# Two graph-attention layers on one core: attention scores computed key-major, denominators by a matmul with ones

## The chip, the cores and the metric

The kernel runs on one core of a Trainium2 chip. A core has a matrix engine (TensorE, "PE" in the profile, with its weight loads listed as "PEld"), a vector engine (VectorE, "DVE"), an activation engine (ScalarE, "ACT"), a general engine (GpSimd, "POOL") and a queue for transfers (SyncE, "SP"). Each engine works through its own instructions in order, and they wait for each other by semaphores. The metric is the device time of one execution in microseconds. Three runs of the kernel before took 3482.77, 3483.33 and 3484.8 us; the median is 3483.33.

## The reference

The input is 64 batches of 256 tokens with 512 features, all in 32-bit floats, and one 256 x 256 adjacency matrix. Layer 0 normalises, takes the positive part, multiplies by the adjacency and by a weight. Layer 1 is attention with 8 heads of 64 features; the mask added to the scores comes from the same adjacency.

```python
def _L0_gnn_ref(x, adj, weight, bias):
    y = jnp.einsum('nm,bmd->bnd', adj, x)
    return jnp.einsum('bnd,do->bno', y, weight) + bias

def _L1_gnn_ref(x, adj, Wq, bq, Wk, bk, Wv, bv, Wo, bo):
    q = (x @ Wq + bq).reshape(b, n, H, HD)
    ...
    scores = jnp.einsum('bqhd,bkhd->bhqk', q, k) / jnp.sqrt(jnp.float32(HD))
    scores = scores + (1.0 - adj)[None, None, :, :] * -1000000000.0
    attn = jax.nn.softmax(scores, axis=-1)
    out = jnp.einsum('bhqk,bkhd->bqhd', attn, v).reshape(b, n, d)
    return out @ Wo + bo

h = jnp.maximum(_layernorm(x, axis=-1), 0.0)
x = x + _L0_gnn_ref(h, adj, L0_gnn_weight, L0_gnn_bias)
h = jnp.maximum(_layernorm(x, axis=-1), 0.0)
x = x + _L1_gnn_ref(h, adj, L1_gnn_Wq, ...)
```

The adjacency is between 0 and 1, not symmetric in its values, and no row is all zero (its diagonal is at least 0.05).

## The kernel before

The 64 batches are taken in 32 groups of two. One group has 512 tokens: four tiles of 128 tokens by 512 features. All weights stay in SBUF.

`pre(g)` is layer 0 and the q, k and v of layer 1 of one group. It loads nothing itself; it takes the group's x tile, computes mean and variance on DVE (`moments`, L120 to L123), the two scales (`norm_scales`, L111 to L118: a tensor-scalar on DVE, a power on POOL, a product on DVE), the normalised positive part `h` on ACT (L134), and adds the bias on POOL (L135). Then come steps that each fill one PSUM bank of 512 columns and are evacuated by ACT or DVE: four `py` (adjacency times h, copied to `yT` by ACT), four `pw` (times the layer-0 weight, added to x by DVE, with the second layer's moments), four `h1` on ACT with four transposes `ph` each and a DVE copy to `h1T`, four `pq`, four `pk` (evacuated by ACT with the bias), and four `pv` (evacuated by DVE). `post(g)` is the output projection: four `po`, each added to `x1` by DVE, and a store for each batch.

Attention works in units: one pair of heads of one batch, eight units in a group. `softmax` (L207 to L229) makes query-major scores `sc`: queries on the partitions, keys along the row, two heads and two query tiles, so 1024 columns in two PSUM banks. The two heads lie on the two 64-partition halves of q and k, so their matmuls use the two row halves of the array. DVE scales and adds the mask (L218), then takes each row's maximum (L221). ACT takes the exponential with that maximum as bias, four instructions of 256 columns, which also give the row sums (L224). DVE takes the reciprocals of the four sums (L227), and POOL multiplies the four blocks by them (L229). `transpose` (L231 to L243) turns the eight 128 x 128 blocks on TensorE, because the product with v needs the keys on the partitions, and copies them from PSUM to `aT`, one head on ACT and one on DVE. `attend` (L245 to L259) multiplies with v; the two heads write the two 64-partition halves of a PSUM bank `pav` (tag `po`), using the two column halves of the array. When both batches of a head pair are in it, DVE copies it to `oT`.

The order is written out in the loop at the end, and a scheduler then places the instructions on each engine, so that neighbouring pieces can interleave. In a group's loop, `softmax` runs two units ahead of `transpose` and `attend`, and between them the generator `fill` is advanced: it holds the steps of `post(g - 1)` followed by those of `pre(g + 1)`. What is left of `fill` runs at the group's end.

PSUM has eight banks: three for the steps (tag `mm`), two for one unit's scores (`sc`), two for the transposes (`tr`), one for `pav` (`po`).

Of the kernel before, what the change touches and what calls it, by code (L numbers as in the profile page):

```python
# [8 lines left out]
F32 = mybir.dt.float32  # L9
AF = mybir.ActivationFunctionType  # L10
ALU = mybir.AluOpType
AX = mybir.AxisListType


@with_exitstack
def kernel(
# [17 lines left out]
    P = 128  # L34
    B, N, D = x.shape
    H, HD = 8, D // 8
    DC = D // P            # chunks of the feature dimension
    NT = N // P            # token tiles of one batch
    GB = 2                 # batches of one group
    T = GB * NT            # token tiles of one group  # L40
    GN = GB * N            # tokens of one group
    NG = B // GB
    HP = H // 2            # head pairs: two heads fill one 128-feature chunk
    EPS = 1e-5
    SCALE = 1.0 / 8.0
    assert (N, D, HD, GN) == (256, 512, 64, 512)

    const = ctx.enter_context(tc.tile_pool(name="const", bufs=1))
    xpool = ctx.enter_context(tc.tile_pool(name="x", bufs=2))
    act = ctx.enter_context(tc.tile_pool(name="act", bufs=1))  # L50
    qkv = ctx.enter_context(tc.tile_pool(name="qkv", bufs=2))
    att = ctx.enter_context(tc.tile_pool(name="att", bufs=2))
    small = ctx.enter_context(tc.tile_pool(name="small", bufs=4))
    psum = ctx.enter_context(tc.tile_pool(name="psum", bufs=1, space=bass.MemoryType.PSUM))
# [11 lines left out]

    def load_weight(w, name):
        t = const.tile([P, DC, D], F32, name=name)
        nc.scalar.dma_start(t, w.rearrange("(c p) o -> p c o", p=P))  # L69
        return t  # L70

    def load_row(b, name):
        t = const.tile([P, D], F32, name=name)
        nc.scalar.dma_start(t, bass.AP(tensor=b.tensor, offset=b.offset, ap=[[0, P], [1, D]]))  # L74
        return t

    def load_column(b, name):
        t = const.tile([P, DC], F32, name=name)
        nc.scalar.dma_start(t, b.rearrange("(c p) -> p c", p=P))  # L79
        return t  # L80

    w0_sb = load_weight(w0, "w0_sb")
    b0_r = load_row(b0, "b0_r")
    wq_sb = load_weight(wq, "wq_sb")
    bq_c = load_column(bq, "bq_c")
    wk_sb = load_weight(wk, "wk_sb")
    bk_c = load_column(bk, "bk_c")
    wv_sb = load_weight(wv, "wv_sb")
    bv_r = load_row(bv, "bv_r")
    wo_sb = load_weight(wo, "wo_sb")  # L90
    bo_r = load_row(bo, "bo_r")
# [5 lines left out]
    nc.vector.memset(mhalf, -0.5)  # L97

    # adjT[m, k, n] = adj[n, k * 128 + m]
    adjT = const.tile([P, NT, N], F32, name="adjT")  # L100
    pa = psum.tile([P, NT, N], F32, tag="mm", name="pa", bufs=3)
# [4 lines left out]
    mask = const.tile([P, NT, N], F32, name="mask")  # L106
    nc.vector.tensor_scalar(mask, adj_sb, -1.0, 1.0, op0=ALU.mult, op1=ALU.add)
    nc.vector.tensor_scalar(mask, mask, -1000000000.0, None, op0=ALU.mult)
    mask_b = mask.rearrange("p t m -> p (t m)")[:, None, :].to_broadcast([P, 2, NT * N])

    def norm_scales(mv, name):  # L111
        """From (mean, variance) of T token tiles: 1 / sqrt(variance + eps), and -mean times that."""
        rs = small.tile([P, T], F32, tag="rs", name=f"rs_{name}")
        nb = small.tile([P, T], F32, tag="nb", name=f"nb_{name}")
        nc.vector.tensor_scalar(rs, mv[:, :, 1], EPS, None, op0=ALU.add)
        nc.gpsimd.tensor_tensor(rs, rs, mhalf, op=ALU.pow)
        nc.vector.scalar_tensor_tensor(nb, mv[:, :, 0], -1.0, rs, op0=ALU.mult, op1=ALU.mult)
        return rs, nb  # L118

    def moments(mv, t, src, name):  # L120
        st = small.tile([P, nc.vector.BN_STATS_DIM], F32, tag="st", name=f"st_{name}_{t}")
        nc.vector.bn_stats(st, src)
        nc.vector.bn_aggr(mv[:, t, :], st)  # L123

    def pre(g):
        """Layer 0 and the q, k and v of layer 1, in steps of one PSUM bank each."""
        xt = XT.pop(g)
        mv = small.tile([P, T, 2], F32, tag="mv", name=f"mv0_{g}")
        for t in range(T):
            moments(mv, t, xt[:, t, :], f"0_{g}")  # L130
        rs, nb = norm_scales(mv, f"0_{g}")
# [3 lines left out]
        nc.gpsimd.tensor_tensor(xt, xt, b0_r[:, None, :].to_broadcast([P, T, D]), op=ALU.add)  # L135

        # yT = (adj @ h) transposed
        yT = act.tile([P, DC, GN], F32, tag="yT", name=f"yT_{g}")
        for d in range(DC):
            ps = psum.tile([P, GN], F32, tag="mm", name=f"py_{g}_{d}", bufs=3)  # L140
            for b in range(GB):
                for k in range(NT):
                    nc.tensor.matmul(ps[:, b * N:(b + 1) * N], h[:, b * NT + k, d * P:(d + 1) * P],  # L143
                                     adjT[:, k, :], start=(k == 0), stop=(k == NT - 1))
            nc.scalar.copy(yT[:, d, :], ps)
            yield
# [3 lines left out]
        for t in range(T):  # L150
            ps = psum.tile([P, D], F32, tag="mm", name=f"pw_{g}_{t}", bufs=3)
# [4 lines left out]
            moments(mv, t, x1[:, t, :], f"1_{g}")  # L156
            yield

        rs, nb = norm_scales(mv, f"1_{g}")
# [106 lines left out]
    for _ in pre(0):  # L266
        pass
# [56 lines left out]
```

## Time and profile before

| what | value |
|---|---|
| runs shown | 3482.77, 3483.33, 3484.8 us |
| profiled execution, span from first to last instruction | 3481.1 us |
| granted TensorE clock, mean | 0.999 |
| POOL, scaling by the reciprocals (L229), 1024 times | 928.2 us busy |
| ACT, exponentials (L224), 1024 times | 507.2 us busy |
| ACT, reading their sums, 1024 times | 191.3 us busy |
| DVE, scale and mask (L218), 256 times | 311.3 us busy |
| DVE, row maxima (L221), 256 times | 309.6 us busy |
| DVE and ACT, copies of the transposes (L243, L241), 256 each | 175.9 and 148.7 us busy |
| DVE, copy of pav to oT (L259), 128 times | 88.6 us busy |
| POOL, bias added to 128 x 2048 (L135, L170), 32 each | 144.7 and 144.6 us busy |
| HBM traffic | 21 GB/s over the span |

The page gives no separate total for the profiled execution; its span is 2.2 us under the median of the runs. Rows of the page name the line, engine, operation, the tiles written and read, shapes, count, then busy time in total, the mean of one in ns, and the idle time before such instructions with who ended it. Matmul records overlap each other, so their mean is longer than the slot that one takes; the spacing of blocks in the chain of waits is the better price. A matmul of 32-bit floats is two records.

### The profile page before, as it was taken

The page shows a single profiled execution, that of the slowest core. Times are in us where ns is not written, and L with a number is a line of the kernel's source. Part 1 is how long each engine was busy: PE and PEld are TensorE (multiplying, and loading weights), DVE is VectorE, ACT ScalarE, POOL GpSimd, SP SyncE. Part 2 cuts the span into 40 slices and gives each one's busy share as a digit, 9 for nine tenths or more (in the row PEclk, how much of TensorE's full clock was granted, in tenths as well). Part 3 has the DMA queues.
Part 4 walks back from the last instruction along what each step waited for, and adds up shares of the span by engine and source line. Part 5 has one row for each costly group of instructions (what it writes and reads, how often), then busy time and mean ns, then how long its engine had stood idle before and what let it go on. Part 6 is the DMA issues. An engine that isn't in the chain of part 4 may idle for free.

```text
span 3481.1 us, 33533 instructions
## 1 busy us (share of the span) xinstructions
PE 3434.9 (99%) x12804; PEld 1774.1 (51%) x12804; DVE 1537.4 (44%) x2308; ACT 1092.9 (31%) x2945; POOL 1281.7 (37%) x1158
## 2 busy tenths in 40 slices
PE   6999999999999999999999999999999999999999
PEld 3555545555455554555545555545555455554554
DVE  1453444444445434455344453444544445434444
ACT  2332323323333233332233322333323333223332
POOL 1443334324334234343333433334424334233333
PEclk9999999999999999999999999999999999999999
DMA  3000000000000000000000000000000000000000
GB/s 109 13 25 13 25 13 25 25 25 13 13 25 25 25 13 19 19 25 25 13 25 13 25 25 16 21 13 25 25 25 13 18 19 25 25 13 19 7 13 25
DMA packets 38863, 75.54 MB, mean 22 GB/s; under 512 B 2736, under 2 KB 2992, under 8 KB 38704
## 3 DMA queue, kind: packets, MB, share of 16 engines
q1 hardware_dynamic: 34304, 67.12, 5.5%
q10 hardware_dynamic: 4400, 6.30, 0.5%
q8 instruction: 101, 1.65, 0.2%
q14 instruction: 58, 0.48, 0.0%
HBM read 39.85 MB, written 33.55 MB: 21 GB/s over the span
## 4 chain that ended last, share of the span: by engine, by line
PE 97%; ACT 1%; POOL 1%; ACTq 1%; issue 0%; DVE 0%; POOLq 0%; DVEq 0%
PE po L196 13%; PE pq L177 13%; PE pv L185 13%; PE pk L177 13%; PE pw L153 13%; PE pav L253 9%; PE sc L213 9%; PE py L143 7%; PE tr L238 6%; PE ph L168 2%; POOL a L229 1%; ACT aT L241 1%; ACTq L69 0%; ACTq L74 0%; ACTq L79 0%
## 5 line engine op out<-in xcount | busy, mean ns | idle before, releaser
L229 POOL TENSOR_SCALAR a<-a,rden 128x256 f32<-128x256 f32 x1024 | 928.2, 926 | 1770.5 <-PE po L196 946.6
L224 ACT ACTIVATE a<-a,nmax 128x256 f32<-128x256 f32 x1024 | 507.2, 496 | 552.6 <-DVE nmax L221 545.4
L196 PE MATMUL po<-wo_sb,oT 128*128 128x512 f32 x1024 | 470.7, 602 | 0.0
L177 PE MATMUL pk<-h1T,wk_sb 128*128 128x512 f32 x1024 | 453.0, 595 | 0.0
L153 PE MATMUL pw<-w_sb,yT 128*128 128x512 f32 x1024 | 453.0, 595 | 0.0
L185 PE MATMUL pv<-wv_sb,h1T 128*128 128x512 f32 x1024 | 453.0, 595 | 0.0
L177 PE MATMUL pq<-h1T,wq_sb 128*128 128x512 f32 x1024 | 449.7, 597 | 0.8 <-DVE h1T L169 0.8
L241 ACT COPY aT<-tr 128x512 f32<-128x512 f32 x256 | 148.7, 581 | 893.5 <-PE tr L238 893.5
L218 DVE SCALAR_TENSOR_TENSOR a<-sc,mask 128x1024 f32<-128x1024 f32 x256 | 311.3, 1216 | 260.4 <-PE sc L213 259.2
L253 PE MATMUL pav<-aT,v 128*64 128x256 f32 x2048 | 355.0, 392 | 9.3 <-ACT aT L241 9.3
L213 PE MATMUL sc<-kT,qT 64*128 64x256 f32 x2048 | 343.2, 407 | 0.0
L177 PEld LDWEIGHTS pq<-h1T,wq_sb 128*128 128x128 f32 x1024 | 192.5, 191 | 243.7 <-issue 230.7
L221 DVE TENSOR_REDUCE nmax<-a 128x4 f32<-128x1024 f32 x256 | 309.6, 1209 | 4.3
L185 PEld LDWEIGHTS pv<-wv_sb,h1T 128*128 128x128 f32 x1024 | 189.6, 190 | 227.1 <-issue 227.1
L177 PEld LDWEIGHTS pk<-h1T,wk_sb 128*128 128x128 f32 x1024 | 189.6, 190 | 225.5 <-issue 215.6
L153 PEld LDWEIGHTS pw<-w_sb,yT 128*128 128x128 f32 x1024 | 189.6, 190 | 225.1 <-issue 217.4
L196 PEld LDWEIGHTS po<-wo_sb,oT 128*128 128x128 f32 x1024 | 183.8, 190 | 213.5 <-issue 213.0
L238 PEld LDWEIGHTS tr<-ident,a 128*128 128x128 f32 x2048 | 231.8, 141 | 109.2 <-issue 82.8
L238 PE MATMUL tr<-ident,a 128*128 128x128 f32 x2048 | 273.0, 276 | 3.7 <-POOL a L229 3.7
L253 PEld LDWEIGHTS pav<-aT,v 128*64 128x64 f32 x2048 | 163.5, 136 | 216.8 <-issue 136.2
L243 DVE COPY aT<-tr 128x512 f32<-128x512 f32 x256 | 175.9, 687 | 219.6 <-PE tr L238 219.6
L213 PEld LDWEIGHTS sc<-kT,qT 64*128 64x128 f32 x2048 | 191.6, 185 | 155.9 <-issue 85.3
(37 smaller groups left out, 2358.3 us busy)
## 6 DMA issues: line engine op xcount, KB each, us to landing
xt<-in_x_dram SPq DMA_DIRECT2D x32, 1024.0 KB, 5.2
out_dram<-x SPq DMA_DIRECT2D x64, 512.0 KB, 2.8
w_sb<-in_L_gnn_weight_dram ACTq DMA_DIRECT2D x1, 1024.0 KB, 11.6
wq_sb<-in_L_gnn_Wq_dram ACTq DMA_DIRECT2D x1, 1024.0 KB, 14.8
wk_sb<-in_L_gnn_Wk_dram ACTq DMA_DIRECT2D x1, 1024.0 KB, 15.5
wv_sb<-in_L_gnn_Wv_dram ACTq DMA_DIRECT2D x1, 1024.0 KB, 10.0
wo_sb<-in_L_gnn_Wo_dram ACTq DMA_DIRECT2D x1, 1024.0 KB, 9.6
adj_sb<-in_adj_dram ACTq DMA_DIRECT2D x1, 256.0 KB, 5.6
```

The source lines that it names most:

```text
L143: nc.tensor.matmul(ps[:, b * N:(b + 1) * N], h[:, b * NT + k, d * P:(d + 1) * P], adjT[:, k, :], start=(k == 0), stop=(k == NT - 1))
L153: nc.tensor.matmul(ps, yT[:, d, t * P:(t + 1) * P], w0_sb[:, d, :], start=(d == 0), stop=(d == DC - 1))
L177: nc.tensor.matmul(ps, w[:, d, m * P:(m + 1) * P], h1T[:, d, :], start=(d == 0), stop=(d == DC - 1))
L185: nc.tensor.matmul(ps, h1T[:, d, t * P:(t + 1) * P], wv_sb[:, d, :], start=(d == 0), stop=(d == DC - 1))
L196: nc.tensor.matmul(ps, oT[:, c, t * P:(t + 1) * P], wo_sb[:, c, :], start=(c == 0), stop=(c == HP - 1))
L213: nc.tensor.matmul(ps[:, j, t * N:(t + 1) * N], Q[g][j * HD:(j + 1) * HD, hp, b * N + t * P:b * N + (t + 1) * P], K[g][j * HD:(j + 1) * HD ...
L218: nc.vector.scalar_tensor_tensor(a.rearrange("p (j t) m -> p j (t m)", j=2), ps, SCALE, mask_b, op0=ALU.mult, op1=ALU.add)
L221: nc.vector.tensor_reduce(nmax, a, AX.X, ALU.max, negate=True)
L224: nc.scalar.activation(a[:, i, :], a[:, i, :], AF.Exp, bias=nmax[:, i:i + 1], accum_out=den[:, i:i + 1])
L229: nc.gpsimd.tensor_scalar(a[:, i, :], a[:, i, :], rden[:, i:i + 1], None, op0=ALU.mult)
L238: nc.tensor.transpose(ps[:, k, t * P:(t + 1) * P], a[:, j * NT + t, k * P:(k + 1) * P], ident)
L253: nc.tensor.matmul(PO[hp][j * HD:(j + 1) * HD, b * N:(b + 1) * N], V[g][:, b * NT + k, h * HD:(h + 1) * HD], aT[:, j, k, :], start=(k == 0 ...
```

## The change

Layer 0, the projections and the weights are computed as before. In the attention:

- `score` makes the scores key-major: keys on the partitions, queries along the row (k is the stationary side, q the moving one). The product with v can read the exponentials directly. `transpose`, its PSUM banks and its copies are gone.
- The row maximum is no longer of the scores. A constant `top`, made once, holds for each query the largest mask value of its row, spread over all partitions. `shift` is the DVE operation of before with the transposed mask, and then a subtraction of `top` on POOL (128 x 1024). `exponent` is one ACT instruction of 1024 columns without sums, and then a POOL addition of the two key tiles (128 x 512).
- `attend` handles both batches of a head pair: eight matmuls with v, over k first and the heads inside, and four matmuls of a 128 x 64 matrix of ones with the added exponentials, which give the denominators in a bank `pden` (tag `pd`), each on the 64 partitions that its head's output has. ACT copies them to SBUF and sums them along the row into `stats`; DVE takes the reciprocal of 128 x 512 values in four pieces; DVE multiplies `pav` by it into `oT`; ACT sums the reciprocals into `stats`.
- The loop goes over head pairs: `softmax` of the next pair, `attend` of this one and `fill` advance in turn, five times. The first pair's `softmax` of a group runs at the end of the group before. `pre` has one more step border.
- PSUM: two banks for the steps, four for scores (two buffers), one `po`, one `pd`. Buffers of `a`: four.
- At the end `stats` is compared with a bound of 1e22; one matmul counts the partitions over it, the count is read into a register, and if it is over zero, `general_path` computes everything again with the row maxima, in a loop over the batches with the instructions of the kernel before.

```diff
-    def softmax(g, u):
-        ...
-        nc.vector.tensor_reduce(nmax, a, AX.X, ALU.max, negate=True)
-        ...
-        for i in range(2 * NT):
-            nc.scalar.activation(a[:, i, :], a[:, i, :], AF.Exp, bias=nmax[:, i:i + 1],
-                                 accum_out=den[:, i:i + 1])
-        ...
-        for i in range(2 * NT):
-            nc.gpsimd.tensor_scalar(a[:, i, :], a[:, i, :], rden[:, i:i + 1], None, op0=ALU.mult)
-    def transpose(g, u):
-        ...
+    maskT = const.tile([P, NT, N], F32, name="maskT")
+    nc.vector.tensor_scalar(maskT, adjT, -1.0, 1.0, op0=ALU.mult, op1=ALU.add)
+    nc.vector.tensor_scalar(maskT, maskT, MASKED, None, op0=ALU.mult)
+    ...
+    top_b = top[:, None, :].to_broadcast([P, 2 * NT, N])
+    def score(g, hp):
+        for b in range(GB):
+            ps = SC[b] = psum.tile([P, 2, NT * N], F32, tag="sc", name=f"sc_{g}_{hp}_{b}", bufs=2)
+            for k in range(NT):
+                for j in range(2):
+                    nc.tensor.matmul(ps[:, j, k * N:(k + 1) * N],
+                                     K[g][j * HD:(j + 1) * HD, hp, b * N + k * P:b * N + (k + 1) * P],
+                                     Q[g][j * HD:(j + 1) * HD, hp, b * N:(b + 1) * N],
+                                     start=True, stop=True)
+    def shift(g, hp, b):
+        a = A[hp, b] = att.tile([P, 2 * NT, N], F32, tag="a", name=f"a_{g}_{hp}_{b}")
+        nc.vector.scalar_tensor_tensor(a.rearrange("p (j k) n -> p j (k n)", j=2), SC.pop(b), SCALE, maskT_b,
+                                       op0=ALU.mult, op1=ALU.add)
+        nc.gpsimd.tensor_tensor(a, a, top_b, op=ALU.subtract)
+    def exponent(g, hp, b):
+        a = A[hp, b]
+        nc.scalar.activation(a, a, AF.Exp)
+        s = AS[hp, b] = att.tile([P, 2, N], F32, tag="as", name=f"as_{g}_{hp}_{b}", bufs=2)
+        a4 = a.rearrange("p (j k) n -> p j k n", j=2)
+        nc.gpsimd.tensor_tensor(s, a4[:, :, 0, :], a4[:, :, 1, :], op=ALU.add)
+    def attend(g, hp):
+        po = psum.tile([P, GN], F32, tag="po", name=f"pav_{g}_{hp}")
+        pd = psum.tile([P, GN], F32, tag="pd", name=f"pden_{g}_{hp}")
+        for b in range(GB):
+            a = A.pop((hp, b))
+            for k in range(NT):
+                for j in range(2):
+                    h = 2 * hp + j
+                    nc.tensor.matmul(po[j * HD:(j + 1) * HD, b * N:(b + 1) * N],
+                                     V[g][:, b * NT + k, h * HD:(h + 1) * HD], a[:, j * NT + k, :],
+                                     start=(k == 0), stop=(k == NT - 1))
+        for b in range(GB):
+            s = AS.pop((hp, b))
             for j in range(2):
+                nc.tensor.matmul(pd[j * HD:(j + 1) * HD, b * N:(b + 1) * N], ones, s[:, j, :],
                                  start=True, stop=True)
+        den = att.tile([P, GN], F32, tag="den", name=f"den_{g}_{hp}", bufs=2)
+        nc.scalar.activation(den, pd, AF.Identity, accum_out=stats[:, 0, i:i + 1])
+        yield
+        rden = att.tile([P, GN], F32, tag="rden", name=f"rden_{g}_{hp}", bufs=2)
+        for c in range(4):
+            nc.vector.reciprocal(rden[:, c * P:(c + 1) * P], den[:, c * P:(c + 1) * P])
+            if c < 3:
+                yield
+        ...
+        nc.vector.tensor_tensor(OT[g][:, hp, :], po, rden, op=ALU.mult)
+        nc.scalar.activation(den, rden, AF.Identity, accum_out=stats[:, 1, i:i + 1])
+        yield
+    def softmax(g, hp):
+        score(g, hp)
+        shift(g, hp, 0)
+        yield
+        shift(g, hp, 1)
+        yield
+        exponent(g, hp, 0)
+        yield
+        yield
+        exponent(g, hp, 1)
+        yield
     for g in range(NG):
         ...
+        for hp in range(HP):
+            nxt = softmax(g, hp + 1) if hp + 1 < HP else iter(())
+            fin = attend(g, hp)
+            for _ in range(5):
+                next(nxt, None)
+                next(fin, None)
                 next(fill, None)
+            next(fill, None)
+            if hp + 1 == HP:
+                for _ in fill:
+                    pass
+        if g + 1 < NG:
+            for _ in softmax(g + 1, 0):
+                pass
+    ...
+    nc.vector.tensor_scalar(bad, stats.rearrange("p s i -> p (s i)"), BOUND, None, op0=ALU.is_gt)
+    ...
+    again = nc.values_load(flag[0:1, 0:1], min_val=0, max_val=P)
+    with tc.If(again > 0):
+        general_path(tc, x, adj, w0, b0, wq, bq, wk, bk, wv, bv, wo, bo, out)
+def general_path(tc, x, adj, w0, b0, wq, bq, wk, bk, wv, bv, wo, bo, out):
+    ...
+        with tc.For_i(0, B, 1) as i:
+            body(i)
```

All PSUM tiles of the steps (`py`, `pw`, `ph`, `pq`, `pk`, `pv`, `po`) have `bufs=2` in place of `bufs=3`.

## The prediction

> **What bounds the kernel now.** I read the page's share line and chain first, to see which engine sets the end; then one steady group as a stage and its chain of waits, to price the attention work on TensorE; then the groups by shape, for the durations of what moves.
>
> ```profile
> span 3481.1 us, 33533 instructions
> PE 3434.9 (99%) x12804; PEld 1774.1 (51%) x12804; DVE 1537.4 (44%) x2308; ACT 1092.9 (31%) x2945; POOL 1281.7 (37%) x1158
> PE 97%; ACT 1%; POOL 1%; ACTq 1%; issue 0%; DVE 0%; POOLq 0%; DVEq 0%
> ```
>
> TensorE is busy throughout and 97% of the chain is its own work: nearly no wait of TensorE exists to be won back, so a gain can come only from fewer TensorE slots, and every wait added is paid in full. One group of two batches, and the chain inside it:
>
> ```profile
> 1002.59:1109.98 107.39, 107.10 (x401) 55.37 (x401) 48.17 (x73) 34.09 (x92) 40.04 (x37) 1.00 0.06 20
> by line: PE po L196 13.3%; PE pw L153 13.0%; PE pk L177 13.0%; PE pv L185 13.0%; PE pq L177 13.0%; PE pav L253 10.0%; PE sc L213 9.3%; PE py L143 6.6%; PE tr L238 6.5%; PE ph L168 1.9%; ACT aT L241 0.6%; issue 0.1%; ACTq L241 0.0%
> 1017.52 1.06 PE sc L213 x8
> 1033.39 1.02 PE pav L253 x8
> 1051.27 0.63 PE sc L213 x2
> 1077.31 0.87 PE tr L238 x8
> 1101.93 1.08 PE pav L253 x4
> ```
>
> The first row's columns are length, then busy time of PE, weight loads, DVE, ACT and POOL, then clock (1.00). A period is 107.39, and it repeats to 0.01 in the next. Of it, sc is 9.3%, pav 10.0%, tr 6.5%: 9.99 + 10.74 + 6.98 = 27.7 us; waits and issue 0.7%, 0.75 us; the rest, 79.0, is projections and layer 0, untouched in size. Two heads on the two halves of the array run at once: 8 records (4 matmuls in two passes each) take 1.06 or 1.02, that is two pairs of 0.43 and two seams of 0.1, while a block broken in two costs 0.63 or 1.08 for its part.
>
> ```profile
> L218 DVE SCALAR_TENSOR_TENSOR a<-sc,mask 128x1024 f32<-128x1024 f32 x256 | 311.3, 1216 | 260.4 <-PE sc L213 259.2 <-POOL a L229 1.2
> L170 POOL TENSOR_TENSOR x<-x,bo_r 128x2048 f32<-128x2048 f32 x32 | 144.6, 4518 | 7.2 <-ACT h L164 7.2
> L116 POOL TENSOR_TENSOR rs<-rs,mhalf 128x4 f32<-128x4 f32 x64 | 66.4, 1038 | 298.3 <-DVE mv L123 252.5 <-DVE rs L115 45.8
> L224 ACT ACTIVATE a<-a,nmax 128x256 f32<-128x256 f32 x1024 | 507.2, 496 | 552.6 <-DVE nmax L221 545.4 <-POOL a L229 2.8
> L145 ACT COPY yT<-py 128x512 f32<-128x512 f32 x128 | 74.3, 580 | 355.4 <-PE py L143 355.4
> L179 ACT ACTIVATE kT<-pk,bk_c 128x512 f32<-128x512 f32 x128 | 87.4, 683 | 252.3 <-PE pk L177 252.3
> L224 ACT ACTIVATION_READ_ACCUMULATOR a<-a,nmax 128x1 f32 x1024 | 191.3, 187 | 0.0
> L115 DVE TENSOR_SCALAR rs<-mv x64: 151/170/3137, 10.4 to 3355.4; 128x4 f32<-128x4 f32 x64
> L227 DVE RECIPROCAL rden<-den x256: 159/178/180, 103.7 to 3462.9; 128x4 f32<-128x4 f32 x128
> ```
>
> The last two rows give minimum, median and maximum in ns. Bases: the span is 3481.1, the runs' median 3483.33, so 2.2 lies around the span; sums are made as differences and added to 3483.
>
> **TensorE's own work.** Per head pair after: sc four pairs 1.73, pav four pairs 1.73, pden (the ones-matmul, two pairs) 0.86, seams 0.23, in all 4.55; times four, 18.2 a group against 27.7. That is 9.5 us a group won if nothing waits. The weight loads (64 columns, 136 ns) stay under the 0.22 slot.
>
> **Prices not shown.** Shift (DVE): the L218 row, 1.22. POOL's subtract, 128x1024: half of L170, 2.26; its add, 128x512: a quarter, 1.13. No row excludes a fixed part: with all of L116's 1.04 as fixed they are 2.78 and 1.91. I take the proportional values (same instruction, nearest size); less than that has no row, since POOL's other elementwise row (128x256 in 926, L229) is dearer per element. Exp over 1024: twice L145 is 1.16, four times L224 is 1.98, one fixed part saved four times over bounds it near 0.95; I take 1.15. The denominators' ACT pass with its sum: 0.68 + 0.19 = 0.87. Reciprocal of 128x128, R: at one element per ns on top of 0.17 it is 0.30; the slowest 128x4 reciprocal (180) less the fastest 128x4 operation (151) spread over four elements is 7.2 ns each, 1.08. The rows sit between, R = 0.8 is a little over the middle; both ends are kept.
>
> [...]
>
> **The waits it adds.** The built order of instructions is the same in every steady group. TensorE: pv; sc of pairs 0 and 1; pav_0; pden_0; four po; py_0; sc_2; pav_1; pden_1; py_1 to py_3; pw_0 to pw_2; sc_3; pav_2; pden_2; pw_3; pden_3; pav_3; ph; pq. Each queue runs in order. Times below count from the named start; a reader starts 0.2 after a block's last slot.
>
> Head, from the end of pv: sc_0 batch 0 ends 0.96; shifts end 2.4 and 3.6, and sc_1, needing those PSUM buffers, ends 4.5; subtract 2.5 to 4.8, exp to 6.0, pav's first batch to 6.9; second subtract to 7.0, exp to 8.2, pav to 9.1. POOL then does add (8.2), pair 1's subtract (10.4), and only then the second add (11.55), so pden_0 ends 12.0. TensorE had 6.25 of work: wait 5.8. Pair 1 behind it is covered by four po (14 us).
>
> Middle: with two mm buffers instead of three py_3 needs py_1 copied, and that copy stands on ACT behind pair 2's second exp and the denominator pass: wait 1.6. Elsewhere a slot of 3.48 covers the 0.69 evacuation.
>
> Tail, from the end of pw_2: DVE finishes pw_2's add and moments at 1.85; shifts to 3.1 and 4.3; subtracts to 5.45 and 7.7; exps to 6.65 and 8.9; adds to 8.85 and 10.05. TensorE has sc_3, pav_2, pden_2, pw_3 until 8.1, then pden_3 until 10.6. pav_3 needs the only po bank, freed by pair 2's product, and that is late: its denominators (PSUM free since 4.5) wait on ACT behind both exps until 8.9, done 9.8; three R to 12.2; pw_3's add 12.9; R 13.7; moments 14.4; product 15.1; pav_3 ends 16.85. Then on DVE aggregate, one R of pair 3 (16.0), rs (16.2); POOL pow 17.4; h1 18.4; four ph gated by h1 at 0.8 each until 21.3; the last h1T copy, behind pair 3's product and other copies, lets pq start at 22.7. TensorE's work in that stretch is 12.65: wait 10.05.
>
> Sum: 79.0 + 18.2 + 5.8 + 1.6 + 10.05 = 114.65 against 107.39: +7.25 a group, times 31 groups, +225.
>
> **Edits with small answers.** The max reduction (309.6), small reciprocals, both aT copies and POOL's scaling leave; DVE, ACT and POOL are at 44, 31 and 37% and off the chain, so this by itself wins 0. Moving the next group's first scores to the end of the previous, and one more step in pre, are in the order above. Constants for `top` lie mostly beside the 13 us in which the first py waits for h: 0 to 3, taken 1. Input loads and stores keep their place on SP; the flag's load stands before the last two stores there and its value is ready earlier: 0. The branch at the end has no row: 0, or at most one x load's 5.2; taken 2. The last group has no next pre to cover or gate it, so I leave the ends equal otherwise. 3483 + 225 + 3 = 3711; rounded down to 3707 because seams saved inside projection blocks (6.87 against 7.06 in the chain) give back a little.
>
> One thing could make it worse: rs (L115) has a median of 170 and a maximum of 3137 ns, when POOL was in its 4.5 us two-input operation. [...] In the tail POOL is idle when rs runs, so the sum takes 0; were rs held by one subtract each group, up to 2.26 x 31 = 70 would be added.
>
> **Rivals.**
> - Reciprocal dear (1.08). The tail pays 5 x 0.28; above R = 0.82 po_2 waits (three R stand before po_0's evacuation), above 0.87 pw_0 waits (four R stand before yT's last copy): 1.4 + 0.8 + 0.85 = 3.05 a group, +95: 3800. For: an operation that has only been seen at four columns. Against: its 178 beside 170.
> - Reciprocal cheap (0.30): 5 x 0.5 = 2.5 less: 3630.
> - The other side: POOL's pieces cost half (1.13, 0.57). The head has three subtracts and two adds in its path, the tail two subtracts: 4.5 + 2.3 = 6.8 less, 210 us; with R under 0.7 the waits fall below the deciding 10.2 a group and it ends near 3465. No row speaks for that rate.
> - The changed order (k outer, head inner) keeps the halves from overlapping: 24 pairs x 0.43 = 10.3 a group, of which perhaps 4 fall into waits: about 3900. Against: sc has this order now and overlaps.
> - The change does not do what it says: the branch is taken. Then a whole second, slower pass follows, over 6900. It needs denominators or reciprocals summing over 1e22, far from layer-normalised scores.
>
> **How the numbers follow.** Forecast 0.40, dear 0.28, cheap 0.20, other side 0.05, no overlap 0.04, branch 0.01, 0.02 none of these. Range: cheap, less 40 for waits counted a microsecond or so too long a group, 3590; dear, plus 0.3 fixed on POOL's pieces (seven of them in the paths, 2.1 x 31 = 65), 3875. Within 0.2% is about what these runs cannot tell from no change. Faster 0.05, same 0.01, slower 0.94.
>
> **What would show it.** The period from pq to pq near 114.7; TensorE's busy share falls to about 85%; no tr; pav 8 records per batch at 0.86 to 1.0; TensorE's longest waits at pav_3 on DVE's product, at ph on h1, at pav_0 and pden_0 on ACT and POOL; the reciprocal's mean; subtract near 2260 ns. Wrong if the reciprocal or the subtract is far off, or if TensorE shows no idle before pav_3.

## The result, and the profile after

The changed kernel takes 3703.6 us (median of four runs, 3702.2 to 3705.1) against 3483.8 beside it: 1.0632 times as long, 95% interval 1.0617 to 1.0647. The forecast was 3707, and its range 3590 to 3875. The page of the profiled execution after, first the shares of the engines, then the chain:

```profile
span 3700.8 us, 28840 instructions
PE 3279.1 (89%) x11784; PEld 1639.6 (44%) x11784; DVE 1366.9 (37%) x2061; ACT 863.1 (23%) x1409; POOL 1265.2 (34%) x646
...
PE 69%; POOL 13%; DVE 12%; ACT 3%; issue 3%; ACTq 0%; DVEq 0%
PE po L366 13%; PE pq L347 12%; PE pk L347 12%; PE pv L355 12%; POOL a L392 10%; PE pw L323 9%; PE sc L383 4%; PE py L313 3%; DVE a L390 3%; DVE rden L424 3%; PE pav L410 3%; POOL as L399 2%; DVE h1T L339 2%; ACT a L396 2%; DVE st L42 1%
```

No engine is busier than before; every one has less to do. But TensorE's part of the chain went from 97% to 69%, and POOL, which had 1%, has 13%, most of it in one line: the subtract, L392. The bound is no longer one engine's work but a chain that goes round POOL, ACT, DVE and back. Two steady groups, stretch by stretch (length, then busy time of PE, weight loads, DVE, ACT, POOL, then clock):

```profile
1072.12:1187.47 115.35, 103.14 (x368) 51.59 (x368) 42.61 (x65) 26.90 (x44) 39.51 (x21) 0.96 0.05 19
1187.47:1300.81 113.34, 100.94 (x368) 50.51 (x369) 42.42 (x65) 26.90 (x44) 39.51 (x21) 0.97 0.05 19
```

Where a group had 107.39 us with 107.10 busy, it now has 114.34 in the mean, of which TensorE stands 12.3 (115.35 - 103.14 and 113.34 - 100.94). The clock column is no longer 1.00, and two equal groups differ by 2 us; both were in no forecast. The chain inside the first of these groups (start, us, what), its head and its tail:

```profile
1113.58 1.09 PE sc L383 x8
...
1114.69 1.24 DVE a L390
...
1118.31 2.35 POOL a L392
1120.67 1.22 POOL as L399
1121.89 1.50 POOL a L392
...
1124.17 1.27 POOL as L399
...
1125.48 0.65 PE pden L416 x4
1126.13 15.63 PE po L366 x32
...
1165.17 0.70 DVE x L325
...
1168.01 1.43 POOL a L392
...
1170.33 2.37 POOL a L392
...
1172.71 1.06 ACT a L396
...
1174.38 2.58 DVE rden L424 x3
...
1178.91 0.60 DVE oT L429
...
1179.55 3.68 PE pav L410 x16
1183.23 1.06 PE ph L338 x4
...
1187.47 0.70 PE pq L347
```

This is the forecast's order, link by link: in the head the subtract, addition, pair 1's subtract and the second addition on POOL before pden_0; in the tail two subtracts, the exp, the denominators, the reciprocals of pair 2, its product, and only then pav_3. The groups of instructions that set the lengths (mean ns after the comma):

```profile
L392 POOL TENSOR_TENSOR a<-a,top 128x1024 f32<-128x1024 f32 x256 | 599.4, 2358 | 1963.1 <-DVE a L390 1953.6 <-DVE rs L51 9.4
...
L424 DVE RECIPROCAL rden<-den 128x128 f32<-128x128 f32 x512 | 446.5, 919 | 652.7 <-ACT den L420 652.7
L399 POOL TENSOR_TENSOR as<-a 128x512 f32<-128x512 f32 x256 | 321.0, 1270 | 0.4 <-ACT h L334 0.4
...
L396 ACT ACTIVATE a<-a 128x1024 f32<-128x1024 f32 x256 | 270.6, 1057 | 1408.9 <-POOL a L392 1408.9
```

And the waits of TensorE (us in total, times, longest):

```profile
PE pav L410 <- DVE oT L429: 111.9, 31, 3.7
PE pav L410 <- ACT a L396: 79.8, 64, 1.3
PE pden L416 <- POOL as L399: 70.1, 33, 2.4
...
PE py L313 <- ACT yT L315: 31.1, 30, 1.0
...
PE pq L347 <- DVE h1T L339: 26.7, 32, 0.9
PE ph L338 <- ACT h L334: 24.8, 34, 5.2
```

The first line is pav_3 in each of the 31 groups, the next two are the head, the fourth is py_3 with its two banks. ACT waited 1408.9 us for POOL's subtract (the L396 row): ACT is not slow, it is fed late.

### The profile page after: what moved, and what is told of

Same layout as the page of the kernel before. It is cut to its first block, busy times and chain, and to the rows that moved or that the text cites. A ratio compares the mean times of both kernels' runs of the same rounds, so it can differ in the third digit from the quotient of the medians.

```text
span 3700.8 us, 28840 instructions
## 1 busy us (share of the span) xinstructions
PE 3279.1 (89%) x11784; PEld 1639.6 (44%) x11784; DVE 1366.9 (37%) x2061; ACT 863.1 (23%) x1409; POOL 1265.2 (34%) x646
## 4 chain that ended last, share of the span: by engine, by line
PE 69%; POOL 13%; DVE 12%; ACT 3%; issue 3%; ACTq 0%; DVEq 0%
PE po L366 13%; PE pq L347 12%; PE pk L347 12%; PE pv L355 12%; POOL a L392 10%; PE pw L323 9%; PE sc L383 4%; PE py L313 3%; DVE a L390 3%; DVE rden L424 3%; PE pav L410 3%; POOL as L399 2%; DVE h1T L339 2%; ACT a L396 2%; DVE st L42 1%
## 5 line engine op out<-in xcount | busy, mean ns | idle before, releaser
L392 POOL TENSOR_TENSOR a<-a,top 128x1024 f32<-128x1024 f32 x256 | 599.4, 2358 | 1963.1 <-DVE a L390 1953.6
L424 DVE RECIPROCAL rden<-den 128x128 f32<-128x128 f32 x512 | 446.5, 919 | 652.7 <-ACT den L420 652.7
L396 ACT ACTIVATE a<-a 128x1024 f32<-128x1024 f32 x256 | 270.6, 1057 | 1408.9 <-POOL a L392 1408.9
L410 PE MATMUL pav<-a,v 128*64 128x256 f32 x2048 | 310.3, 449 | 191.7 <-DVE oT L429 111.9
L390 DVE SCALAR_TENSOR_TENSOR a<-sc,maskT 128x1024 f32<-128x1024 f32 x256 | 301.0, 1217 | 63.1 <-PE sc L383 59.7
L399 POOL TENSOR_TENSOR as<-a 128x512 f32<-128x512 f32 x256 | 321.0, 1270 | 0.4 <-ACT h L334 0.4
L410 PEld LDWEIGHTS pav<-a,v 128*64 128x64 f32 x2048 | 153.4, 158 | 328.5 <-DVE oT L429 126.4
L383 PE MATMUL sc<-qT,kT 64*128 64x256 f32 x2048 | 264.3, 392 | 14.8 <-DVE a L390 14.8
L313 PE MATMUL py<-adjT,h 128*128 128x256 f32 x1024 | 244.6, 388 | 36.4 <-ACT yT L315 31.1
L383 PEld LDWEIGHTS sc<-qT,kT 64*128 64x128 f32 x2048 | 184.5, 186 | 115.7 <-issue 59.6
```

The costliest lines, as they stand in the source:

```text
L383: nc.tensor.matmul(ps[:, j, k * N:(k + 1) * N], K[g][j * HD:(j + 1) * HD, hp, b * N + k * P:b * N + (k + 1) * P], Q[g][j * HD:(j + 1) * HD ...
L390: nc.vector.scalar_tensor_tensor(a.rearrange("p (j k) n -> p j (k n)", j=2), SC.pop(b), SCALE, maskT_b, op0=ALU.mult, op1=ALU.add)
L392: nc.gpsimd.tensor_tensor(a, a, top_b, op=ALU.subtract)
L396: nc.scalar.activation(a, a, AF.Exp)
L399: nc.gpsimd.tensor_tensor(s, a4[:, :, 0, :], a4[:, :, 1, :], op=ALU.add)
L410: nc.tensor.matmul(po[j * HD:(j + 1) * HD, b * N:(b + 1) * N], V[g][:, b * NT + k, h * HD:(h + 1) * HD], a[:, j * NT + k, :], start=(k == ...
```

## The experiments

Theory A is the forecast's: TensorE's own work fell, and more than that comes back as waits on a chain of POOL, ACT and DVE. Against it stood that TensorE's clock is the loss, that the reciprocal is, that the PSUM banks are, and that the removal was worth little. One table for all, for steady groups: "idle" is length less TensorE's busy time; "slow" is its busy time over 98.5, which is what the same matmuls take with the clock at 1.00 (the last row); a stretch at half clock makes it grow (po took 15.63 with the clock at 0.89 and 13.93 at 1.00 in the changed kernel), and so do added matmuls. Both come from the stretches' rows, one to four groups of each run. "Folded" means that `top` is subtracted from the mask once, ahead of the loop.

| run | time, us | ratio to before (95%) | group, us | idle | slow |
|---|---|---|---|---|---|
| changed kernel | 3703.6 | 1.0632 (1.0617 to 1.0647) | 114.3 | 12.3 | 3.5 |
| top folded into the mask | 3420.3 | 0.9818 (0.9805 to 0.9832) | 105.8 | 5.2 | 2.1 |
| half of it folded | 3593.9 | 1.0311 (1.0294 to 1.0328) | 110.9 | 7.8 | 4.6 |
| three extra matmuls | 3662.8 | 1.0514 (1.0500 to 1.0528) | 112.8 | 10.1 | 4.2, of it 2.6 extra |
| fold, two extra matmuls | 3352.8 | 0.9621 (0.9608 to 0.9634) | 103.4 | 3.5 | 1.4, with two extra matmuls in it |
| banks dealt otherwise | 3619.8 | 1.0389 (1.0373 to 1.0404) | 112.1 | 8.2 | 5.3 |
| no reciprocal | 3761.0 | 1.0795 (1.0779 to 1.0812) | 116.0 | 13.5 | 4.0 |
| no addition on POOL | 3752.3 | 1.0771 (1.0753 to 1.0789) | 116.1 | 9.7 | 7.8, of it 3.4 ones |
| scales per token tile | 3701.8 | 1.0626 (1.0610 to 1.0642) | 114.3 | 10.1 | 5.7 |
| the same, three extra matmuls | 3743.1 | 1.0743 (1.0726 to 1.0761) | 116.9 | 9.5 | 8.8, of it 2.6 extra |
| fold and scales per tile | 3260.0 | 0.9360 (0.9348 to 0.9373) | 100.5 | 2.0 | 0.0 |

### The removal by itself

In the kernel before:

```diff
-        aT = ATT[u] = att.tile([P, 2, NT, N], F32, tag="aT", name=f"aT_{g}_{u}")
-        for j in range(2):
-            ... (8 transposes, 2 copies)
+        ATT[u] = a.rearrange("p (j k) n -> p j k n", j=2)
```

> The kernel before with the 8 transposes of each unit and their two copies left out; the product with v reads the query-major exponentials as they are, so it computes another thing with the same amount of work. Theory A (the transposes stood on TensorE's path, with nothing under them): 6.98 of tr and the 0.4 to 0.75 of waits on the copies a group, 32 groups: 3484 - 32 x 7.5 = 3245, range 3200 to 3265. Rival (removing work lets another engine become the bound: POOL's scaling of 29 us and its bias additions of 9 a group stand at 37%, DVE's at 44%): between 3300 and 3484, with waits of TensorE on POOL or DVE of several us a group.

Measured: 3213.2 us, 0.9222 times before (0.9208 to 0.9236). A steady group:

```profile
1031.73:1130.27 98.54, 97.10 (x337) 47.46 (x337) 39.73 (x65) 29.79 (x85) 40.01 (x37) 1.00 0.06 22
```

The group is 8.85 shorter and 97.10 of its 98.54 are busy: the transposes stood on TensorE's path, and POOL with 40 us a group stays under it. The time is 32 under theory A's 3245, inside its range; the rival falls. Of the 8.85, tr and the waits of the group before make 7.7; where the other 1.1 comes from was not measured apart. So some 270 us were there to be won, and the loss after has another source than a small gain.

### POOL's subtract, whole and half

```diff
-        nc.gpsimd.tensor_tensor(a, a, top_b, op=ALU.subtract)          # in shift
+    for k in range(NT):                                                # once, ahead of the loop
+        nc.vector.tensor_tensor(maskT[:, k, :], maskT[:, k, :], top, op=ALU.subtract)
```

> The constant top is subtracted from the transposed mask once, ahead of the loop, and POOL's subtract over 128x1024 is gone; all results stay the same and the order of the other instructions too. Theory A (the waits of the prediction: POOL's subtracts stand in the head's and the tail's path): the head has three subtracts ahead of pden_0, 3 x 2.36 = 7.1, of which no more than the wait of 6.3 can go, and the exps then follow DVE's shifts, so about 5 goes; the tail has two, 2 x 2.36 = 4.7, of which ACT's queue gives back a little, about 4. Period 114.3 - 9 = 105.3, time 3704 - 31 x 9 = about 3425, range 3380 to 3480: faster than both kernels. Theory B (the half clock after idle windows is most of the loss, and the windows stay): 3600 to 3660. Theory C (POOL's subtract lies beside other waits, as ACT and DVE chains end as late): 3690 to 3704. The records at half clock should fall from 293 us to under 100 by A.

And half of it, the mask of key tile 0 alone:

```diff
+    nc.vector.tensor_tensor(maskT[:, 0, :], maskT[:, 0, :], top, op=ALU.subtract)
-        nc.gpsimd.tensor_tensor(a, a, top_b, op=ALU.subtract)
+        nc.gpsimd.tensor_tensor(a4[:, :, 1, :], a4[:, :, 1, :], top_b, op=ALU.subtract)
```

> Half of POOL's subtract: top is folded into the mask for the first key tile only, and POOL subtracts it from the 512 columns of the second (1.27 by the addition of the same size, in place of 2.36). All values the same. Theory A (the subtract stands in the path with its whole length, in the head three times and in the tail twice): half of what the whole fold gave, 3704 - 142 = 3562, range 3530 to 3600; five times the saved 1.09 is 5.45 a group, 169, which gives 3535. Rival (the first half of the saving is what counts and other waits decide then): under 3490. Rival (a threshold, the gain comes only when POOL's queue has slack): over 3640.

Measured: 3420.3 for the whole, 3593.9 for the half. TensorE's order is the same in all three; DVE and ACT have a few instructions of the tail in another order. Without the subtract the changed kernel is 1.8% faster than the one before, and theory A's 3425 is met to 5 us; the rivals that put the loss elsewhere (3600 and more) fall. That it is met so closely is in part luck. The group lost 8.5 us: the head (first scores to po) 5.2, where 5 were expected; the tail (pair 3's scores to pq) 2.9, where 4 were; the middle, with py_3's wait, 1.3 and a half-clock stretch in po 0.85, which were not in the expectation; and the projections got 1.7 longer, since the half-clock stretch now lies in pq. The half gave 110 of the 283 us, in theory A's range, but less than half. The table says why: idle fell by 4.5 a group, near the 5.45 that five shorter subtracts give, but TensorE's work got 1.1 slower. In the head, for one, a half-clock stretch (985.6 to 989.0) now falls on pav_0 and pden_0, so it takes 12.0 us where it took 12.6, and 7.4 with the whole fold. One expectation was wrong: with the whole fold the time at half clock was to fall under 100 us, and it fell from 293 only to 215 (the sum of the clock's records at 0.50).

### The clock

In the changed kernel, and, with two in place of three, in the one with the fold:

```diff
         nc.scalar.activation(den, pd, AF.Identity, accum_out=stats[:, 0, i:i + 1])
+        if hp + 1 == HP:
+            for _ in range(3):
+                nc.tensor.matmul(pd[0:HD, :], ones, w0_sb[:, 0, :], start=True, stop=True)
```

> Only an addition: three matmuls of ones with a weight (64x512 each, result not used) into the bank of pair 3's denominators after ACT has read it, so that TensorE has work in its wait for pair 2's product; everything else and its order stays. Theory A (waits alone decide, the clock does not matter): 3704, or up to 60 more if the extra matmuls (1.75 each at full clock) push pav_3. Theory B (the half clock after that wait costs: pav_3 took 3.68 instead of 1.95, and ph after it is at half clock): pav_3 back near 1.95 and ph's records shorter, 1.5 to 3 us a group, 31 groups: 3610 to 3660.

> The kernel with top folded into the mask, and two extra matmuls (64x512 each, result not used, 0.87 each at full clock) behind pair 3's denominators. In the run with the fold alone TensorE stands 0.90 before pav_3 and 2.54 before ph (it waits for h1 on ACT), and the half-clock window of 6.83 that follows has 5.6 us of ph and pq in it in every group. The extra matmuls fall into these two waits and can delay pav_3 by a microsecond at most, which the 2.54 behind it take up; ph's own start doesn't depend on them. Theory A (the window follows the idle time, and costs half of the work in it): ph starts as before, the window goes, 2 to 2.8 a group won, 3420 - 31 x 2.4 = 3346, range 3333 to 3385. Rival (the window has another cause, or its cost is hidden in the wait for h1T behind it): 3420, or up to 3450 if the extra work pushes ph.

On every engine the order of a steady group is that of the kernel it started from, but for the extra matmuls, of which the last stands behind pav_3. At full clock one takes 0.87, as po's 16 matmuls of as many columns took 13.93 with the clock at 1.00; the first expectation had twice that. Measured: 3662.8 against 3703.6, and 3352.8 against 3420.3. Adding work to the bounding engine made both kernels faster, by 41 and 67 us. A group of the fold alone, and the half-clock stretch in it, then a group of the fold with two extra matmuls (columns as above):

```profile
989.92:1095.75 105.83, 100.68 (x369) 51.41 (x369) 42.62 (x65) 27.65 (x44) 21.08 (x13) 0.97 0.06 20
...
1092.34:1099.17 6.83, 5.64 (x14) 3.09 (x13) 5.02 (x12) 1.80 (x4) 5.46 (x2) 0.50 0.00 0
```

```profile
976.72:1080.14 103.42, 99.92 (x373) 50.73 (x373) 43.15 (x65) 27.31 (x44) 21.07 (x13) 1.00 0.06 21
```

With four more records the group is 2.4 shorter, because the 6.83 us at 0.50 are gone. That is the 2.4 expected: in these two runs the half clock behind the wait cost 2.4 us a group, and work in the wait kept it away. On the changed kernel itself the gain is 3 us short of the range expected: one half-clock stretch of 3.41 is left in 27 of 30 groups, in the head or in the tail, and in 22 groups pav_3 still waits up to 0.9 for the product.

### Scales per token tile

```diff
-        rs, nb = norm_scales(nc, small, mhalf, mv, f"1_{g}")
+            sc1.append(norm_scales(nc, small, mhalf, mv[:, t:t + 1, :], f"1_{g}_{t}"))   # in pw's loop
```

> Only the chain to h1 is changed: the second layer norm's two scales are made for each of the four token tiles as its moments come, in place of one time for all four after the last; the same values come out. POOL's power (1.04) is then 4 a group in place of 1 and h1 of the first three tiles doesn't wait for pw_3. Theory A (pav_3's wait for pair 2's product stands in front and keeps most of the tail; ph can start earlier and fill part of it): 1 to 2 us a group, 3640 to 3685. Rival 'the h1 chain is the tail': the waits at ph of 0.9 and the serial h1 and ph of 0.8 each go, 4 us a group: 3580. Rival 'no effect': 3704.

Measured: 3701.8, no change. It lets three of the four ph move ahead of the end of pden_3 and of pav_3 on TensorE. Two groups, row by row:

```profile
958.60:1074.04 115.44, 105.44 (x369) 52.68 (x368) 44.49 (x72) 27.74 (x46) 42.81 (x24) 0.94 0.05 19
1074.04:1187.27 113.23, 103.03 (x369) 51.55 (x369) 42.19 (x69) 26.40 (x42) 38.66 (x23) 0.97 0.05 19
```

Idle time is 10.1 where it was 12.3, but busy time is 104.2 where it was 102.0: the 2.2 saved came back as slower work, and the half-clock stretches of the run add up to 348 us in place of 293. Stage by stage (means of 24 groups) the tail is 0.8 shorter, 21.4 for 22.2, and po 0.8 longer, as it now has a half-clock stretch in every group and not in every second. The clock is not all of it: on DVE three copies to h1T now stand ahead of pair 2's product, which ends 16.8 us after pw_2 and not 14.4, so the tail had less to win than the expectation gave it. To test the clock's part, the tail was kept busy as above:

> The scales per token tile, and the three extra matmuls (result not used) behind pair 3's denominators, both on the changed kernel without the fold. The scales alone cut TensorE's idle time from 407 to 343 us, and the time stayed within 2 us, while the busy time in half-clock windows rose from 214 to 304 us. Theory A (the shorter waits were real, and the clock's half windows took the gain back): with the tail kept warm the windows fall to about 110 us and 60 to 100 us come back: 3605 to 3660. Rival (the shorter waits don't reach the end whatever the clock): 3660 to 3700, as the extra matmuls alone made 3663. Rival (the extra matmuls push the tail): over 3700.

Measured: 3743.1, so the third case, and no proof of theory A. In the built order the extra matmuls stood behind three of the four ph, so the waits ahead of those (0.82 and 1.72) were as before, the clock fell, and the extra matmuls themselves ran at half of it: in one group the end of pden_3 and the extra matmuls took 7.2 us, in another 4.1 (three extra ones take 2.6 at full clock). In these runs extra work helped in the gap and not behind it. How much of this edit's gain the clock took back, and how much the later product, no run shows apart.

With both the fold and the scales per tile:

> Both at once: top folded into the mask, and the scales per token tile; all values the same. In the run with the fold alone the longest waits left are at ph for h1 (3.1 a group) and at pav_3 (0.9), and one window of 6.83 at half clock follows the wait at ph in every group, with up to 2.8 lost in it. Theory A (those are what is left): the h1 of three tiles is early, ph's wait goes but for about 1, and the half window with it: 105.8 - 2 - 2.5 = 101 to 103 a group, time 3265 to 3345. Rival (the wait only moves to pav_3 or pq, and the window stays): 3380 to 3420.

Measured: 3260.0, 0.936 times before (0.9348 to 0.9373), 5 us under theory A's range: the fastest version here that computes the same. Its page and a group:

```profile
span 3257.7 us, 28869 instructions
PE 3161.8 (97%) x11784; PEld 1613.1 (50%) x11784; DVE 1389.2 (43%) x2255; ACT 885.6 (27%) x1409; POOL 713.8 (22%) x486
PE 84%; DVE 12%; ACT 2%; issue 1%; ACTq 1%; POOL 0%; DVEq 0%; POOLq 0%
```

```profile
947.91:1048.42 100.51, 98.54 (x368) 50.30 (x368) 43.18 (x71) 27.65 (x44) 22.29 (x16) 1.00 0.06 21
```

The edit that gave 2 us on the changed kernel gives 160 here. Idle fell by 3.2 a group and slow work by 2.1, which is 5.3 x 31 = 164.

### The reciprocal, the addition, the banks

```diff
-            nc.vector.reciprocal(rden[:, c * P:(c + 1) * P], den[:, c * P:(c + 1) * P])
+            nc.vector.tensor_tensor(rden[:, c * P:(c + 1) * P], den[:, c * P:(c + 1) * P],
+                                    den[:, c * P:(c + 1) * P], op=ALU.max)
```

> The four reciprocals of 128x128 (0.86 to 0.92 each) are replaced by the maximum of the denominators with themselves, so the product uses denominators where reciprocals belong; nothing else is changed in the program, but the built order moves with it: pair 2's product comes ahead of pw_3's addition, and four statistics passes of the next group's x (0.69 each) come ahead of the rs of this group. Rival 'reciprocal cheap' of the prediction, by its own sum (five reciprocals in the tail's path, here 5 x 0.6 = 3.0 a group): 3704 - 93 = 3610. Theory A (the wait for the product at pav_3 goes, 3.7, and comes back at ph, since h1 now waits behind the passes that have moved up): 3680 to 3715. A theory by which the clock's half windows follow the longest wait leaves 3700 too, with the long wait at ph.

Measured: 3761.0. Slower than with the reciprocals, and outside all that was expected. The piece fell from 919 to 412 ns, and the chain from denominators to product from 4.5 to 1.6 us; TensorE's waits then:

```profile
PE ph L338 <- ACT h L334: 55.0, 34, 5.2
...
PE pq L347 <- DVE h1T L339: 31.0, 32, 4.7
PE ph L338 <- DVE h1T L339: 23.8, 29, 0.8
...
PE pq L347 <- ACT qT L349: 13.0, 29, 0.5
PE pw L323 <- ACT yT L315: 10.8, 30, 0.4
```

pav_3 now stands ahead of pden_3, so pden_3's pass over the denominators stands on ACT ahead of h1, and ph waits 54 us more in all; the wait ahead of pav_3 fell only from 4.8 (1.06 and 3.71) to 3.4 a group. What the tail won is nearly gone at ph: from pair 3's scores to pq a group is 0.4 shorter. Elsewhere it is longer: po by 0.7, with a half-clock stretch in every group instead of every second; the stretch from py to pair 3's scores by 0.6 and the projections by 0.7, where the small waits at pw and pq are new. Since the order moved with the edit, the run does not say what a cheaper reciprocal in the same order would give; it does say that in this order the product's earlier start was not worth 3 us.

The addition, left to TensorE:

```diff
-        nc.gpsimd.tensor_tensor(s, a4[:, :, 0, :], a4[:, :, 1, :], op=ALU.add)
-                nc.tensor.matmul(pd[...], ones, s[:, j, :], start=True, stop=True)
+            for k in range(NT):
+                    nc.tensor.matmul(pd[...], ones, a[:, j * NT + k, :], start=(k == 0), stop=(k == NT - 1))
```

> POOL's additions of the key tiles are gone; the ones-matmul reads both key tiles of the exponentials instead, eight matmuls in place of four for a head pair. All values the same. TensorE has 0.86 x 4 = 3.4 a group more work. Theory A (the additions stand in the path at the head and the tail alone, the subtracts and the product decide more): the head's pden_0 no longer waits for the second addition (about 2 won net of its own 0.86), pairs 1 and 2 pay 0.86 each, the tail wins at most 1.2 and pays 0.86: 0 to 1 a group won, 3675 to 3710. Rival (POOL's whole queue is the loss, whichever operation): 1.27 x 3 + less won, 3 a group: about 3610.

Measured: 3752.3, 42 over the end of theory A's range. Idle fell by 2.6 a group, 3.4 was added, and the rest, 0.9, is slow work that the expectation had left out. The 2 us to be won in the head did not come: it takes 12.6 as before, since a half-clock stretch (1020.9 to 1024.3 in one group) now falls on its pav and pden. The rival (POOL's whole queue, 3 a group won net) falls: the additions are not worth their length.

```diff
-            ps = SC[b] = psum.tile([P, 2, NT * N], F32, tag="sc", ..., bufs=2)
+            ps = SC[b] = psum.tile([P, 2, NT * N], F32, tag="sc", ..., bufs=1)
-        po = psum.tile([P, GN], F32, tag="po", name=f"pav_{g}_{hp}")
+        po = psum.tile([P, GN], F32, tag="po", name=f"pav_{g}_{hp}", bufs=2)     # and mm: 3 in place of 2
```

> The changed kernel with PSUM dealt out otherwise: one score buffer in place of two, three banks for the steps in place of two, two banks for pav in place of one. All results stay. Theory A (the waits at py_3 and pav_3 come from missing banks, the head's and the h1 chain do not): py_3's 1.5 goes, pav_3's wait of 3.7 goes but most of it comes back at ph, which waits for h1 behind the same DVE queue; the single score buffer adds waits at sc of the second batch. Period 110 to 113, time 3570 to 3660. Rival (banks are the main cause of the tail): period under 107, under 3480. Rival (the score buffers matter more than the others): 3704 or slower.

Measured: 3619.8, in theory A's range. The wait at pav_3 for the product is gone, and ph's wait for h1 went from 24.8 to 94.2 us in all. The order moved here too, and the banks of three tags were changed at once, so what each is worth is not shown. Together they are worth 84 us, the subtract 283. That the banks decide where the chain is waited for, and the subtract how long it is, is a reading of these rows.

## Why the prediction was right, point by point

- **TensorE's own work, 79.0 + 18.2 = 97.2.** 98.5, by the run with fold and scales per tile. The direction was right, the term 1.3 too small; in its chain the blocks of pair 1 and 2 in the middle take 1.93 (sc), 1.88 (pav) and 0.86 (pden), 4.67 against the forecast 4.55. That makes 0.5 of it; the rest is open.
- **Waits, 5.8 + 1.6 + 10.05 = 17.45.** Idle is 12.3, by stretch 5.1, 1.0 and 6.1 in one group; 3.5 is slow work, together 15.8. The terms were right in place, and the stretches nearly in length, since much of the slow work lies in the tail. Head, from pv's end to po: 12.55 against 12.0. Middle: py_3 waits 1.0 against 1.6. Tail, from pw_2's end to pq: 22.32 against 22.7. But 0.85 of the slow work lies in po (15.63 and 13.93 in turn), where the forecast had no wait.
- **What failed inside the tail.** The product ends at 14.4 after pw_2 (forecast 15.1) and pav_3 then takes 3.68 (forecast 1.75), at clock 0.50. ph starts when pav_3 ends, at 18.1, and not when h1 comes (forecast 18.4); the first h1 ended at 17.4 by the trace. So the forecast's 22.7 stands on a pav_3 at full clock and an h1 that is a microsecond later than it was. The stretch held because 1.9 us of half clock took the place of a wait. The clock is the step that the working did not have.
- **Luck in the sum.** Against the forecast's 114.65 a group has 5.15 less idle time, 3.5 of slow work that was not in it, and 1.3 more of TensorE's own work: 114.3. The chain and the places of its waits were forecast; that the total came within 4 us of 3707 is a balance of errors. The upper end of the range is a slip of addition: 3800 + 65 is 3865, not 3875, which decides nothing here.
- **Prices.** Shift 1.22 (1.22); subtract 2.36 (2.26); addition 1.27 (1.13); exp 1.06 (1.15); denominators' pass 0.58 + 0.19 = 0.78 (0.87); reciprocal 0.86 from one to the next, three in 2.58 (0.80). Those that had two ends lay between them. The rival's "above R = 0.82 po_2 waits" did not come: po waits 0.3 us in the whole run.
- **rs behind POOL.** Mean 220 ns, the longest 364: in the steady groups it never meets a subtract, and 29 of the 64 meet only the last third of a microsecond of POOL's bias addition. So the term 0 was right. Where rs met that addition it ended with it, as the last section shows, but that cost next to nothing in this kernel.
- **The ends.** The first pq starts at 54.3 (before 54.8), and from the last pq to the end there are 113.1 (before 114.4): the constants and the branch cost nothing that shows; 3 was allowed.
- **Busy share near 85%.** 89%: by 98.5 / 114.3 it would be 86%, the half-clock work counts as busy.
- **Rivals.** No overlap of halves and the branch are excluded by the profile (pav_1's sixteen records take 1.88 us, and no second pass follows). POOL at half price was the other side; the run with half the subtract came near that case and gave 3594, not 3465, as the additions kept their length (1.27), and the slow work rose from 3.5 to 4.6 a group.

## What to carry to other kernels

Where one engine is 99% busy, price a change by what it saves there and by every wait it puts into the same engine's queue: here 270 us of transposes were won and a constant's subtraction on POOL, off that engine, cost 283. A subtraction of a constant from a sum with another constant belongs into that constant. And a wait of TensorE cost more than its length here where the clock fell behind it (6.83 us at 0.50 behind the wait in the run with the fold, 2.4 us a group), so what an edit to one wait is worth depends on the waits that are left: the scales per token tile gave 2 us on the changed kernel and 160 on the one with the fold.

## What the runs showed of the hardware

In the changed kernel's trace the 52 stretches at clock 0.50 lie on a grid: from the first start, 47.88, to the last, 3700.15, are 1070.0 steps of 3.413, and each of the others starts a whole number of steps behind the first. Three of them start at 1126.50, 1177.70 and 1290.34, 15.0 and 33.0 steps apart; in the steady groups a stretch lasts one step or two (3.41 or 6.83 us). Three whole steps of the grid, and the half-clock stretch behind the first of them:

```profile
1174.28:1177.70 3.42, 1.30 (x8) 0.42 (x8) 3.32 (x5) 0.75 (x3) 0.85 (x1) 1.00 0.00 0
1177.70:1184.53 6.83, 4.98 (x23) 3.08 (x24) 5.64 (x11) 2.40 (x5) 1.02 (x1) 0.50 0.45 154
...
1286.92:1290.34 3.42, 1.50 (x9) 0.42 (x8) 2.28 (x3) 1.80 (x5) 1.89 (x2) 1.00 0.00 0
...
1239.14:1242.55 3.41, 1.70 (x7) 0.83 (x8) 0.00 (x0) 1.06 (x1) 3.41 (x3) 1.00 0.02 5
```

The steps at 1174.28 and 1286.92, with TensorE busy 38% and 44%, are each followed by 6.83 us at 0.50; the one at 1239.14, with 50%, is not. Over all such steps of this run from 24 us on, where the records of the clock begin, with the matmul records laid on the grid, 52 were followed by half clock: 51 have at most 0.44 busy and one, in the last group, 0.46. Those that were not followed have at least 0.49. In other runs the border is less sharp: with the three extra matmuls nine steps at 0.44 were not followed while four between 0.51 and 0.58 were, and in the kernel without transposes five at 0.65 were, and others at 0.65 were not. So in these runs the busy time by records nearly tells the steps that were followed from the others, but not fully. The grid does not follow the groups: two of them make 228.69 us, 67.0 steps, so one has 33.5, and equal groups take 115.35 and 113.34 in turn, one with a half-clock step at the start of po and the other without.

On POOL an operation with two inputs took 1270 ns for 128x512 and 2358 for 128x1024: 2.1 ns a column and some 0.18 us fixed, neither of the forecast's ends. A reciprocal of 128x128 has a spacing of 0.86 us against the 178 ns of 128x4 before: (860 - 178) / 124, some 5.5 ns for each further column, or 6.0 by its mean record of 919.

In these traces the small rs on DVE (128x4, 0.11 to 0.17 us where it met none in the kernels before and after) ended only with the POOL operation of two large inputs that it met. In the kernel before, 30 of the 64 began within POOL's bias addition of 4.5 us; they took 3.13 us, and each ended 0.02 after it. In the changed kernel 29 began some 0.3 before its end and ended with it. With the banks dealt otherwise one met a subtract at its start and took 2.34 us, the subtract's length; an nb (128x4) early in the changed kernel met one too and took 2.30. In the run without the reciprocal 29 met the addition and took 2.85. Larger operations of DVE kept their lengths: in the changed kernel the 160 shifts that overlap a subtract took 1.21 to 1.23, as their mean of 1.217, and the reciprocals beside any operation of POOL 0.89 to 0.95.
